# Scores' leaky relu into a PSUM bank, a new order of work by pairs of graphs, and a three-bank Strassen product in a four-layer graph attention kernel

## The chip, the cores and the metric

The kernel runs on one core of one Trainium2 chip. Its time is the device time of one launch in microseconds, the median of three runs. A profiled execution, taken by the hardware profiler, gives the views that are read below.

## The reference

128 independent graphs (`B = 128`) of 128 nodes each, with 512 features in float32, pass through four attention layers. Each layer adds its result to its input and normalises every row (`x = layernorm(x + layer(x))`). Layer 0 is plain attention on the features. Layer 1 has two parts: one with four heads over `x @ W1` (512 to 1024 columns) and an elu, and one with a single head over `h @ W2` (1024 to 512 columns). Layer 2 has eight heads over `x @ W` (512 columns). Layer 3 is attention on the features again. The scores of every attention have the same form:

```python
scores = leaky_relu(s_src[:, :, None] + s_dst[:, None, :], 0.2)
scores = where(adj == 0, -inf, scores)
attn   = softmax(scores)
out    = attn @ features
```

## The kernel before

**One graph fills the 128 partitions.** A graph is a tile of 128 x 512 floats. For each of them the kernel emits the same list of operations: `first` (layer 0), a projection by `W1`, `second` (the four heads), a share in the product by `W2` (`halves`), and `third` (the rest of layer 1, layer 2 and layer 3). All arithmetic is float32, and each float32 matmul appears in the trace as two records.

**An attention** is built of helpers. `spread` (L589 to L596) turns a column of scores into a row by way of DRAM and lays it out on all partitions: one write by SP, one read by SP. `attend` then runs, for each head, `prelu` on ScalarE (L646: leaky relu of row plus column, into the SBUF tile `z`), `masked` on VectorE (L654: the negated minimum of `z` plus a mask, with the row's minimum in `nm`), `exp` on ScalarE (L663, with the row's sum) and one reciprocal (L671). Some attentions are scaled on GpSimd (L673). `turned` (L607 to L622) transposes the result in blocks of 32 x 32 on VectorE and finishes the transposition by a write to DRAM and a read from it on SP's queue. Only then can TensorE use it: `mixed` (L725) for one head, L896 and L938 for several. Per graph there are six calls of `attend` with 1, 4, 1, 4, 4 and 1 heads, so 15 of each head's instruction. In the trace all SBUF tiles of 128, 512 or 1024 floats are named `w`, all PSUM banks `ps`.

**The product by W2** is done for two graphs at once by Strassen's scheme, with seven block products for eight. It uses four PSUM banks `pa` to `pd`, four evictions by ScalarE (L807) and four additions on VectorE (L812) for each pair; the sums of blocks are made on GpSimd (L780). Half of it is emitted with the odd graph of a pair and half with the even graph of the next pair.

**The order of the work** is set at build time. `plan` places one graph's operations in a cyclic timetable of `PERIOD = 28` us from rough costs (a DMA counts 7.06 us in it). `order` then runs a list scheduler over all graphs: on each engine it takes the operation that can start first, no further ahead than `AHEAD = 20` us of due time, and hands out PSUM banks (at most 8) and SBUF buffers by its own clock. Each engine, SP's DMA queue included, executes the resulting list strictly in order. The preparation of the weights (L295 to L560) is part of the same list, with due times up to 205 us.

Of the kernel before, what the change touches and what calls it, by code (L numbers as in the profile page):

```python
# [26 lines left out]

PERIOD = 28.0
LATENCY = {"PE": (0.0, 0.8), "DVE": (0.15, 1.44), "ACT": (0.1, 1.44), "POOL": (0.1, 1.44), "SP": (7.06, 7.06)}
FLOW = {"PE": (0.0, 0.6), "DVE": (0.15, 0.8), "ACT": (0.1, 0.8), "POOL": (0.1, 0.8), "SP": (4.5, 4.5)}
AHEAD = 20.0
URGENCY = 0.6
BANKS = 8

SEED, SPREAD = 989, 8.0


class Buf:


    def __init__(self, tag, shape, dtype=F32):
        self.tag, self.shape, self.dtype = tag, shape, dtype
        self.size = 1
        for d in shape[1:]:
            self.size *= d

        if dtype is F32 and shape[0] == P and self.size in (P, 4 * P, 8 * P) and not tag.startswith(("ps", "scr")):  # L50
            self.tag = f"w{self.size}"
        self.ap = self.slot = None

# [7 lines left out]
class Op:  # L61
    def __init__(self, engine, cost, emit, ins, outs, extra, uses=(), dma=0.0):
        self.dma = dma
        self.engine, self.cost, self.emit, self.extra = engine, cost, emit, extra
        self.wait = 0
        self.ins, self.outs = ins, outs
        self.uses = list(uses)
        self.bufs = list(dict.fromkeys([*ins, *outs, *uses]))

    def done(self, reader=None):  # L70
        own, other = LATENCY[self.engine]
        return self.cost + self.extra + (own if reader is self.engine else other)


class Pipeline:
    def __init__(self, make, n, place):
        self.make, self.n, self.place = make, n, place

    def plan(self, ops):


        before, after = [set() for _ in ops], [[] for _ in ops]
        last, readers = {}, {}
        for k, op in enumerate(ops):
            for b in op.ins:
                before[k].add(last[b])
            for b in op.outs:
                if b in last:
                    before[k].add(last[b])
                before[k].update(readers.get(b, ()))  # L90
            before[k].discard(k)
            for q in before[k]:
                after[q].append(k)
            for b in op.ins:
                readers.setdefault(b, set()).add(k)
            for b in op.outs:
                last[b], readers[b] = k, set()
        left = [0.0] * len(ops)
        for k in reversed(range(len(ops))):
            left[k] = ops[k].cost + max(  # L100
                (left[q] + ops[k].done(ops[q].engine) - ops[k].cost for q in after[k]), default=0.0
            )
        taken = {e: [] for e in LATENCY}
        times, ready, missing = [0.0] * len(ops), [0.0] * len(ops), [len(q) for q in before]
        waiting = [k for k in range(len(ops)) if not missing[k]]
        rng = random.Random(SEED)
        shift = [SPREAD * rng.random() for _ in ops]
        while waiting:
            k = min(waiting, key=lambda k: (ready[k] - URGENCY * left[k] + shift[k], k))
            waiting.remove(k)  # L110
            op, t = ops[k], ready[k]
            spans = taken[op.engine]
            while True:
                u = t % PERIOD
                clash = [
                    y + d - u for x, y in spans for d in (-PERIOD, 0.0, PERIOD)
                    if u < y + d - 1e-9 and x + d < u + op.cost - 1e-9
                ]
                if not clash:
                    break  # L120
                t += min(clash) + 1e-9
                assert t < ready[k] + 2 * PERIOD, "the period is too short"
            spans.append((t % PERIOD, t % PERIOD + op.cost))
            times[k] = t
            for q in after[k]:
                ready[q] = max(ready[q], t + op.done(ops[q].engine) + max(ops[q].wait, 0) * PERIOD)
                missing[q] -= 1
                if not missing[q]:
                    waiting.append(q)
        return times  # L130

    def run(self, setup):
        times, events = self.plan(self.make(None)), [(t, -1, k, op) for k, (t, op) in enumerate(setup)]
        for g in range(self.n):
            for k, op in enumerate(self.make(g)):
                if op is not None:
                    events.append((g * PERIOD + times[k], g, k, op))
        events.sort(key=lambda e: e[:3])
        for g, op in self.order(events):
            for b in op.outs:  # L140
                if b.ap is None and b.slot is not None:
                    b.ap = self.place(b, g)
            op.emit()

    def order(self, events):

        ops, n = [e[3] for e in events], len(events)
        ends, first, last, readers, open_uses = {}, {}, {}, {}, {}
        before, after = [0] * n, [[] for _ in ops]
        makes, coming = [[] for _ in ops], {}  # L150
        for i, op in enumerate(ops):
            need = {last[b] for b in op.ins + op.uses if b in last}
            for b in op.outs:
                need.update([last[b]] if b in last else [], readers.get(b, ()))
                if b not in first:
                    first[b] = events[i][0]
                    if b.tag != "const":
                        makes[i].append(b)
                        coming.setdefault(b.tag, []).append(i)
            need.discard(i)  # L160
            before[i] = len(need)
            for q in need:
                after[q].append(i)
            for b in op.ins + op.uses:
                readers.setdefault(b, []).append(i)
            for b in op.outs:
                last[b], readers[b] = i, []
            for b in op.bufs:
                open_uses[b] = open_uses.get(b, 0) + 1
                ends[b] = max(ends.get(b, 0.0), events[i][0] + op.done())  # L170

        free = {}
        for b, t in first.items():
            if b.tag != "const":
                places = free.setdefault(b.tag, [])
                s = next((s for s, e in enumerate(places) if e <= t), len(places))
                places[s : s + 1] = [ends[b]]
        assert len(free["ps"]) <= BANKS, "too few banks"
        free = {tag: [(0.0, s) for s in range(BANKS if tag == "ps" else len(p))] for tag, p in free.items()}
        ready, released, clock, lane = [0.0] * n, {}, {e: 0.0 for e in FLOW}, 0.0  # L180
        known = {e: [i for i in range(n) if not before[i] and ops[i].engine == e] for e in FLOW}
        issued, low, out = [False] * n, 0, []

        def start(i):
            t = max(clock[ops[i].engine], ready[i])
            for b in makes[i]:

                rank = 0
                for q in coming[b.tag]:
                    if q >= i or rank >= len(free[b.tag]):  # L190
                        break
                    rank += 1
                if rank >= len(free[b.tag]):
                    return None
                t = max(t, free[b.tag][rank][0])
            return t

        while len(out) < n:
            best = None
            for e, waiting in known.items():  # L200
                found = None
                for i in waiting:
                    if events[i][0] > events[low][0] + AHEAD and i != low:
                        break
                    t = start(i)
                    if t is not None and (found is None or t < found[0]):
                        found = (t, i)
                        if t <= clock[e]:
                            break
                if found and (best is None or found < best):  # L210
                    best = found
            t, i = best
            op = ops[i]
            known[op.engine].remove(i)
            issued[i] = True
# [6 lines left out]
            if op.engine == "POOL":  # L222
                other += op.extra
# [20 lines left out]
def tile_gat_stack(  # L244
# [86 lines left out]
    def spread_row(t, r, a):  # L331
# [5 lines left out]
        return b  # L337

# [700 lines left out]
```

## Time and profile before

| | before |
|---|---|
| median of 3 runs | 3231.36 us (3228.59 to 3233.77) |
| span of the profiled execution | 3258.4 us |
| instructions | 62058 |
| PE busy | 3066.8 us (94%) |
| DVE busy | 2779.0 us (85%) |
| ACT busy | 2451.2 us (75%) |
| POOL busy | 1895.1 us (58%) |
| DMA engines, mean | 186 GB/s |

The page gives no other time for the profiled execution than its span, which is 27 us (0.8%) above the median of the runs shown. PE is TensorE's matmuls, PEld its loads of weights, DVE is VectorE, ACT ScalarE, POOL GpSimd, SP the queue that issues nearly all transfers.

### The profile page before, as it was taken

The page shows a single profiled execution, that of the slowest core. Times are in us where ns is not written, and L with a number is a line of the kernel's source. Part 1 is how long each engine was busy: PE and PEld are TensorE (multiplying, and loading weights), DVE is VectorE, ACT ScalarE, POOL GpSimd, SP SyncE. Part 2 cuts the span into 40 slices and gives each one's busy share as a digit, 9 for nine tenths or more (in the row PEclk, how much of TensorE's full clock was granted, in tenths as well). Part 3 has the DMA queues.
Part 4 walks back from the last instruction along what each step waited for, and adds up shares of the span by engine and source line. Part 5 has one row for each costly group of instructions (what it writes and reads, how often), then busy time and mean ns, then how long its engine had stood idle before and what let it go on. Part 6 is the DMA issues. An engine that isn't in the chain of part 4 may idle for free. (4 is left out here: it accounts for less than half of the span.)

```text
span 3258.4 us, 62058 instructions
## 1 busy us (share of the span) xinstructions
PE 3066.8 (94%) x14822; PEld 2488.7 (76%) x14822; DVE 2779.0 (85%) x9833; ACT 2451.2 (75%) x8741; POOL 1895.1 (58%) x2347
## 2 busy tenths in 40 slices
PE   6899999999999999999999999999999999999984
PEld 4688887787777877877777778777787777878853
DVE  4779888888888988898888889889898898989875
ACT  2457787787777777787777877777877777778875
POOL 4655655665565655665555665565566556565533
PEclk7899999999999999999999999999999999999985
DMA  4358777877877877877778777877787787777875
GB/s 119 94 136 196 183 205 188 200 193 190 203 187 188 205 186 192 201 190 200 188 187 200 191 188 204 189 190 201 191 204 187 188 205 188 196 196 190 197 174 129
DMA packets 1657567, 606.08 MB, mean 186 GB/s; under 512 B 1311562, under 2 KB 1508170, under 8 KB 1657204
## 3 DMA queue, kind: packets, MB, share of 16 engines
q1 hardware_dynamic: 1655836, 598.97, 75.0%
q8 instruction: 120, 1.97, 0.2%
q14 instruction: 243, 1.99, 0.2%
q0 software_dynamic: 576, 2.10, 0.2%
q10 hardware_dynamic: 792, 1.06, 0.1%
HBM read 374.43 MB, written 227.48 MB: 185 GB/s over the span
## 5 line engine op out<-in xcount | busy, mean ns | idle before, releaser
L710 PE MATMUL ps<-w1s,w 128*128 128x258 f32 x4096 | 926.9, 384 | 48.5 <-DMA w<-scr 25.0
L710 PEld LDWEIGHTS ps<-w1s,w 128*128 128x128 f32 x4096 | 777.0, 191 | 186.3 <-DVE xl L812 39.5
L654 DVE CUSTOM_DVE_ANT_0 w<-w,w 128x128 f32<-128x128 f32 x1920 | 861.1, 544 | 65.6 <-ACT w L646 49.2
L794 PE MATMUL ps<-w2s,w 128*128 128x257 f32 x3584 | 849.0, 383 | 8.5 <-POOL w L780 8.4
L663 ACT ACTIVATE w<-w,nm 128x128 f32<-128x128 f32 x1920 | 748.0, 394 | 98.2 <-DVE nm L654 76.3
L794 PEld LDWEIGHTS ps<-w2s,w 128*128 128x128 f32 x3584 | 669.1, 191 | 188.8 <-issue 80.0
L646 ACT ACTIVATE w<-w,xl 128x128 f32<-128x128 f32 x1536 | 488.8, 389 | 279.9 <-DMA w<-row 259.1
L607 DVE STREAM_TRANSPOSE w<-w 128x512 f32<-128x512 f32 (+1 forms) x1024 | 551.5, 540 | 34.3 <-ACT w L663 13.3
L710 PE MATMUL ps<-wha,w 128*128 128x273 f32 x2048 | 502.3, 398 | 7.3 <-DMA w<-scr 6.9
L710 PEld LDWEIGHTS ps<-wha,w 128*128 128x128 f32 x2048 | 383.2, 192 | 87.4 <-DVE w L607 6.3
L699 ACT ACTIVATE w<-w,mr,rd 128x512 f32<-128x512 f32 x512 | 415.2, 811 | 33.9 <-POOL mr L692 33.0
L692 POOL TENSOR_SCALAR mr<-mv,rd 128x1 f32<-128x1 f32 x512 | 160.1, 313 | 409.4 <-ACT rd L686 201.8
L663 ACT ACTIVATION_READ_ACCUMULATOR w<-w,nm 128x1 f32 x1920 | 368.1, 192 | 0.0
L681 DVE BATCH_NORM_STATS2 st<-w 128x6 f32<-128x512 f32 x512 | 337.2, 668 | 5.4 <-POOL w L986 4.6
L881 POOL TENSOR_TENSOR xl<-xl,b1t 128x512 f32<-128x512 f32 x256 | 335.2, 1310 | 1.6
L938 PEld LDWEIGHTS ps<-xl,w 128*128 128x128 f32 x2048 | 274.3, 196 | 80.8 <-issue 24.4
L646 ACT ACTIVATE w<-w,sc 128x128 f32<-128x128 f32 x384 | 152.3, 397 | 227.6 <-DMA w<-row 226.6
L725 PE MATMUL ps<-w,w 128*128 128x512 f32 x512 | 277.4, 624 | 32.6 <-DMA w<-scr 31.6
L738 POOL TENSOR_SCALAR w<-adj 128x128 f32<-128x128 int32 x256 | 192.4, 752 | 188.2 <-DMA adj<-in_adj_dram 75.1
L717 ACT COPY xl<-ps 128x258 f32<-128x258 f32 (+1 forms) x768 | 273.2, 362 | 31.8 <-PE ps L710 31.3
L938 PE MATMUL ps<-xl,w 128*128 128x66 f32 x2048 | 265.2, 273 | 27.7 <-DMA w<-scr 14.4
L654 DVE DVE_READ_ACCUMULATOR2_ANT nm<- 128x1 f32 x1920 | 290.5, 151 | 0.0
(213 smaller groups left out, 4258.8 us busy)
## 6 DMA issues: line engine op xcount, KB each, us to landing
scr<-w SPq DMA_DIRECT2D x640, 256.0 KB
w<-scr SPq DMA_DIRECT2D x640, 256.0 KB
w<-row SPq DMA_DIRECT2D x128, 512.0 KB
w<-in_x_dram SPq DMA_DIRECT2D x128, 256.0 KB
w<-row SPq DMA_DIRECT2D x128, 256.0 KB
out_dram<-w SPq DMA_DIRECT2D x128, 256.0 KB
w<-row SPq DMA_DIRECT2D x384, 64.0 KB
scr<-w SPq DMA_DIRECT2D x384, 64.0 KB
```

Of the source, the lines that this page charges most:

```text
L607: op("DVE", 0.12 + 0.133 * n, lambda: nc.vector.transpose(zb.ap.rearrange("p b h c -> p h b c"), src.ap.rearrange("p (h b c) -> p h b c", ...
L646: nc.scalar.activation(z.ap[:, h, :], db.ap[:, h0 + h, :], AF.Prelu, bias=src(h0 + h), alpha=SLOPE)
L654: nc.vector.tensor_tensor_reduce(out=zz.ap[:, h, :].rearrange("p (b a) -> p a b", b=4), in0=z.ap[:, h, :].rearrange("p (a b) -> p a b", b= ...
L663: nc.scalar.activation(zz.ap[:, h, :], zz.ap[:, h, :], AF.Exp, bias=nm.ap[:, h : h + 1], scale=-1.0, accum_out=rs.ap[:, h : h + 1],)
L681: op("DVE", 0.6, lambda: nc.vector.bn_stats(st.ap, y.ap), [y], [st])
L699: op("ACT", 0.7, lambda: nc.scalar.activation(y.ap, y.ap, AF.Identity, bias=mr.ap, scale=rd.ap), [y, rd, mr], [y])
L710: op("PE", w * 4 / 2400 + 0.006, lambda k=k: nc.tensor.matmul(px.ap[:, :w], lhsT=lhs.ap[:, k, :], rhs=wa(k, c), start=(k == 0), stop=(k == ...
L717: op("ACT", 0.06 + w / 1200, lambda: nc.scalar.copy(dst(), px.ap[:, :w]), [px], [t])
L725: op("PE", width * 4 / 2400, lambda: nc.tensor.matmul(pa.ap[:, :width] if len(xv.shape) == 2 else pa.ap.rearrange("p (s c) -> p s c", s=2) ...
L794: return lambda: nc.tensor.matmul(q[b].ap[:, :C2], lhsT=x()[:, k, :], rhs=w2s[:, slot, k, :], start=(fresh and k == 0), stop=(k == 3), ski ...
L881: op("POOL", 1.3, lambda nh=nh: nc.gpsimd.tensor_add(xl.ap[:, nh, : 2 * FH], xl.ap[:, nh, : 2 * FH], b1t[:, nh * 2 * FH : (nh + 1) * 2 * F ...
L938: op("PE", 0.225, lambda u=u, h=h: nc.tensor.matmul(pa.ap[:, u * CH : (u + 1) * CH], lhsT=pt.ap[:, u, :], rhs=xl3.ap[:, h * CH : (h + 1) * ...
```

## The change

The change rewrites the scheduler and regroups the kernel by pairs of graphs. The arithmetic of the reference is the same. Its parts:

- `attend` writes the leaky relu to a PSUM bank (`z = bank()`), one bank for up to four heads, so that `masked` reads one operand from PSUM and the mask from SBUF.
- `strassen` takes the place of `halves`: the product by `W2` is emitted in one piece for a pair. `pa` accumulates on through four of the seven products, `pb` and `pc` take the rest. Three evictions and one final copy are on ScalarE, three additions on VectorE.
- `pair` emits two graphs together: both `first`, both projections, both `second`, one `strassen`, both `third`, both layer-2 projections, both `fourth`. The second graph of a pair is given a lag of half a period.
- `plan` and `lay_out` take the place of the class `Pipeline`. They have other costs: the four matmuls of one accumulation are one operation, a transfer lands 1.7 + 0.6 us plus its own transfer time after its issue, at most 8 transfers are in flight, and VectorE operations marked `port` and GpSimd operations exclude each other. Due times are 49 us apart for each pair, and the scheduler looks 60 us ahead.
- The preparation of the weights has due times up to 111 us instead of 205 us.
- Small ones: `exp(h - 1)` of the elu is written in place of a tile of its own, and the last attention reads its transposed weights by the other of the two layouts in `turned`.

```diff
-PERIOD = 28.0
-LATENCY = {"PE": (0.0, 0.8), "DVE": (0.15, 1.44), "ACT": (0.1, 1.44), "POOL": (0.1, 1.44), "SP": (7.06, 7.06)}
-FLOW = {"PE": (0.0, 0.6), "DVE": (0.15, 0.8), "ACT": (0.1, 0.8), "POOL": (0.1, 0.8), "SP": (4.5, 4.5)}
-AHEAD = 20.0
-SEED, SPREAD = 989, 8.0
+PERIOD, PACE, AHEAD = 51, 49, 60
+HOP = {'PE': 0.5, 'DVE': 0.5, 'ACT': 0.5, 'POOL': 0.5, 'SP': 1.0}
+URGENCY, SEED, SPREAD = 0.6, 56445, 16.0
+BANKS, PRODUCTS = 8, 2
+FLIGHT, LANDS = 1.7, 0.6
+LANES = 8
...
-            z, zz, nm, rs, ri = (Buf(f"{t}{nh}", s) for t, s in (
-                ("z", [P, nh, P]), ("zz", [P, nh, P]), ("nm", [P, nh]), ("rs", [P, nh]),
-                ("ri", [P, nh])))
-            def prelu():
-                for h in range(nh):
-                    nc.scalar.activation(
-                        z.ap[:, h, :], db.ap[:, h0 + h, :], AF.Prelu, bias=src(h0 + h), alpha=SLOPE
-                    )
+        zz, nm, rs, ri = (Buf(f"{t}{nh}", s) for t, s in (
+            ("zz", [P, nh, P]), ("nm", [P, nh]), ("rs", [P, nh]), ("ri", [P, nh])))
+        z = bank()
+        zh = lambda h: z.ap[:, h * P : (h + 1) * P]
+
+        def prelu():
+            for h in range(nh):
+                nc.scalar.activation(zh(h), db.ap[:, h0 + h, :], AF.Prelu, bias=src(h0 + h), alpha=SLOPE)
...
                     nc.vector.tensor_tensor_reduce(
                         out=zz.ap[:, h, :].rearrange("p (b a) -> p a b", b=4),
-                        in0=z.ap[:, h, :].rearrange("p (a b) -> p a b", b=4),
+                        in0=zh(h).rearrange("p (a b) -> p a b", b=4),
...
+        product(pa, left[0][0], 0, True)
+        taken(pa, t1)
+        product(pc, left[0][1], 1, True)
+        added(pc, t1, 0, 0)
+        product(pa, s[1], 4, False)
+        product(pb, s[0], 3, True)
+        taken(pa, u2)
+        taken(pb, v)
+        product(pa, s[2], 5, False)
+        product(pb, s[3], 2, False)
+        added(pa, v, 1, 1)
+        added(pb, u2, 0, 1)
+        product(pa, left[1][1], 6, False)
+        copied(pa, wide, lambda: to(1, 0), joins=[out[1]])
...
+    def pair(n):
+        a, b = 2 * n, 2 * n + 1
+        sts = [first(a)]
+        k = len(ops)
+        sts.append(first(b))
+        for o in ops[k:]:
+            o.lag = PERIOD / 2
+        xl = [Buf("xl1", [P, 2, N1]) for _ in range(2)]
...
+        hT = [second(st, t) for st, t in zip(sts, xl)]
+        xl2 = [Buf("xl2", [P, 2, C2]) for _ in range(2)]
+        left = [[(t, lambda t=t: t.ap) for t in both] for both in hT]
+        strassen(left, sums(left, [P, 4, P]), w2s, 4, C2, slice(0, C2), lambda g, h: xl2[g].ap[:, h, :], xl2, w2_ready)
+        for g, st, t in zip((a, b), sts, xl2):
+            third(g, st, t)
...
+        for g, st, t in zip((a, b), sts, xl3):
+            fourth(g, st, t)
+
+    pairs = B // 2
+    offsets = None
+    for n in range(pairs):
+        begin = len(ops)
+        pair(n)
+        if offsets is None:
+            own = ops[begin:]
+            offsets = plan(own)
+        for o, t in zip(ops[begin:], offsets):
+            o.due = n * PACE + t
```

## The prediction

> **What bounds the kernel now.** I read the table of stages first, for where TensorE stands still.
>
> ```profile
> core 0: us, PE busy (x) PEld busy (x) DVE busy (x) ACT busy (x) POOL busy (x), PEclk, DMA share, GB/s
> 0.00:163.00 163.00, 124.17 (x448) 87.71 (x449) 97.80 (x287) 58.26 (x178) 96.65 (x103) 0.83 0.40 106
> 163.00:326.00 163.00, 160.80 (x794) 134.71 (x793) 134.21 (x439) 111.63 (x393) 89.05 (x102) 1.00 0.68 166
> 326.00:3095.00 2769.00, 2677.55 (x13201) 2191.98 (x13200) 2435.47 (x8692) 2172.62 (x7797) 1655.09 (x2056) 1.00 0.79 194
> 3095.00:3258.00 163.00, 104.26 (x383) 74.28 (x381) 111.52 (x419) 108.67 (x377) 54.27 (x87) 0.71 0.63 152
> ```
>
> A graph needs 115 matmul records (32 for W1, 28 for W2, 16 for layer 2, 16 and 16 for the heads, 6 for the three single-head attentions, one transpose). So the long stage, with 13201 records, holds 114.8 graphs: **24.12 us a graph, of which PE is busy 23.32 and idle 0.80**. The other engines have more slack (DVE 21.2 us, ACT 18.9, POOL 14.4 a graph). The kernel is bound by TensorE, and what an order of work can win is the 91.5 us of PE idle in this stage and what stands at the ends: 38.8 us of idle in the first 163 us, 2.2 in the second and 58.7 in the last, where the granted clock is also low (0.83 and 0.71).
>
> Next, the waits of PE in the long stage (line, releaser: total, times, longest):
>
> ```profile
> PE ps L710 <- DMA w<-scr: 25.0, 24, 2.1
> PE ps L725 <- DMA w<-scr: 15.2, 27, 1.3
> PE ps L850 <- DVE w L903: 15.0, 15, 1.9
> PE ps L710 <- DVE ri L671: 10.1, 10, 2.1
> PE ps L710 <- DVE st L681: 8.4, 5, 2.0
> PE ps L725 <- ACT w L663: 4.5, 6, 1.0
> PE ps L725 <- ACT xl L717: 4.1, 10, 0.7
> ```
>
> With four smaller rows, transfers end 40.2 us of it, DVE 36.6, ACT 10.1, POOL 1.4: 0.35, 0.32, 0.09 and 0.01 us a graph.
>
> Last, whether DVE works at its own speed. The group of the masked minimum, then one burst of it on the timeline with the GpSimd operation beside it:
>
> ```profile
> L654 DVE CUSTOM_DVE_ANT_0 w<-w,w 128x128 f32<-128x128 f32 x1920 | 861.1, 544 | 65.6 <-ACT w L646 49.2 <-DMA row<-w 11.2 <-ACT w L663 3.8
> ```
> ```profile
> L654 DVE CUSTOM_DVE_ANT_0 w<-w,w x1722: 328/383/1522, 325.9 to 3095.0; 128x128 f32<-128x128 f32 x192
> ```
> ```profile
> 1502.43 1.04 POOL L673 TENSOR_TENSOR w<-w,ri 128x512 f32<-128x512 f32 x1
> 1502.56 1.16 DVE L654 CUSTOM_DVE_ANT_0 w<-w,w 128x128 f32<-128x128 f32 x1
> ...
> 1503.57 0.15 DVE L654 DVE_READ_ACCUMULATOR2_ANT nm<- 128x1 f32 x1
> 1503.57 0.39 DVE L654 CUSTOM_DVE_ANT_0 w<-w,w 128x128 f32<-128x128 f32 x1
> ```
>
> The mean is 544 ns, the median 383, the longest 1522. The first head here took 1.16 us; it was let go when the GpSimd multiplication that began just before it ended (1503.47). The next one took 0.39.
>
> [...] No ACT write to PSUM is in this trace.
>
> **The change part by part.** (1) *prelu to PSUM*: 1920 instructions that took 389 to 397 ns. [...] ACT is idle 22% of the long stage, and 306.6 us of its waits before L646 from 800 to 2600 us are for the row transfer, so nothing reaches the end from this alone.
>
> (2) *Masked minimum from PSUM*: 1920 instructions lose the blocking, 544 - 383 = 161 ns each: -309 us of DVE. [...] I take -250, DVE at some 2500 us with (3). GpSimd is no longer blocked by these either: the masks from `adj` have a mean of 752 ns against a least of 645 (256 of them, 27 us), `mr` 313 against 254 (512, 30 us): up to -57 us of POOL, some of it due to DVE operations that keep two SBUF inputs (L744, L959). Neither engine bounds. What is bought is latency: DVE's 36.6 us of PE idle shrinks, and exp, the transpose and the transfer behind each masked minimum start earlier.
>
> (3) *Three-bank Strassen*: seven products as before, so 3584 records and the same PE time. Four evictions by ACT stay four (three and the last copy); DVE's four additions become three: 64 x 404 ns = -26 us, hidden. `pa` is now read three times between products that add to it; each read (359 ns on ACT, 404 on DVE) has another bank's product beside it, 8 records in 1.9 us on the timeline. Taken at nothing; if the order put no product between, 3 x 64 x 0.4 = +77 us. One bank of four is returned. The score tile takes one: a four-head burst of prelu and minimum ran from 1501.55 to 1504.42, so 3 x 2.9 and about 3 x 1 us a graph, half a bank on average. These cancel.
>
> (4) *SP's queue and the transfers*: the same 30 issues a graph: 8 writes and 8 reads of `turned`, 5 of each of `spread`, x, adj twice, out. At the medians of the trace (432, 429 to 639, 538, 423 ns) that is about 15 us of 24. The bytes stay, so their share goes from 0.79 to about 0.81 when the same work takes 2% less. All issues are moved past each other, and one that waits for its source holds all behind it: that is the risk in rival B.
>
> (5) *The order*: this is where time is won or lost. Of the 0.80 us a graph I expect the DVE part to fall from 0.32 to 0.08 by (2) and a scheduler that knows which operations exclude each other; the transfers from 0.35 to 0.14, as it prices each by its size and looks 60 us ahead, not 20; ACT and POOL stay at 0.08. Idle 0.30, pace 23.62: 0.50 x 115 = -57 us. At the head PE stood 9.0 us before 40 us, waiting for a mask, and 5.7 and 5.0 us at about 120 to 130 for a transfer and a block sum; with more work within reach I take -20 us of the 99.7 at the ends. The tail hardly moves: after the last Strassen two layers hang on single transfers (5.77, 3.86, 2.57 us on the chain that ended last), whatever the order. Bounds for the ends: -50 to +40 (two graphs now reach the tail together, and the second of a pair starts half a period late).
>
> Sum: -57 - 20 = -77 us on the span of 3258.4, so 3181. The median is 27 us below the span; I carry that difference over: **3155 us**. That is -2.4%; about 0.2% is what a measurement of this kernel can tell from no change.
>
> **The rivals.** *A, forecast*: 3155, chance 0.64. Its own range is 3090 (all 91.5 us of the long stage and 50 of the ends gone) to 3224.
>
> *B, the order trusts transfers that land too early* (slower). A row for eight heads is priced at 1.7 + 0.6 + 1.52 = 3.8 us from its issue; the chain at the end shows 5.77 in a stage where the engines are less busy. The narrow ones are priced right (3.96 against 3.86, 2.7 against 2.57). All engines run in order, so a row 2 us late holds ACT, and what is queued behind it, then `turned` and PE's next heads or projection. If two of a graph's thirteen transfers to SBUF that gate an engine are late by 2 us with a third of it uncovered, it is 2 x 2 x 0.33 = 1.3 us of idle a graph where A has 0.14 for transfers: pace 24.12 + (1.3 - 0.35) - 0.26 (A's gain on the other waits) = 24.81, +79 us on 115 graphs, less 10 at the head: 3300. It decides once PE's idle exceeds 0.97 us a graph (0.80 plus the 20 us of the ends). For it: `ACT w L646 <- DMA w<-row` is already the longest wait. Against: PE still ran at 97% with it. Chance 0.30.
>
> *C, no change*: DVE's relief is real, but every wait of PE that it shortens is followed by one for a transfer that lands no sooner (L710 already waits 24 times for `scr`, 1 us each), so the idle 0.80 us stays and is only put down to other releasers: 3225 to 3238. Chance 0.06.
>
> **How the numbers follow.** Faster 0.64, same 0.06, slower 0.30. The range runs from A's low end to B's value: 3090 to 3300.
>
> **What would show it.** Right: in the long stage 0.2 to 0.4 us of PE idle a graph; the masked minimum (now with `ps` as input) with a mean near 400 and its longest under 700 ns; DVE busy near 2500 us; still 3584 records of W2. Wrong: PE waits for `scr` or `row` transfers above 60 us, or a pace above 24.1. [...] if it falls and the pace doesn't, C holds.

## The result and the profile after

The kernel after takes **3494.3 us** (median, 3492.5 to 3499.3) beside 3230.0 for the kernel before on the same chip: a ratio of **1.084 [1.081, 1.087]**, slower by 264 us where 77 us less was forecast. The profiled execution has a span of 3490.5 us, 4 below the median.

The table of stages, cut as it was for the kernel before (first and second 163 us, the long stage, the last 163 us; columns in the first line, "x" counts instructions):

```profile
core 0: us, PE busy (x) PEld busy (x) DVE busy (x) ACT busy (x) POOL busy (x), PEclk, DMA share, GB/s
0.00:163.00 163.00, 124.72 (x442) 89.94 (x443) 92.29 (x290) 58.04 (x177) 92.98 (x102) 0.87 0.39 107
163.00:326.00 163.00, 153.43 (x719) 122.37 (x718) 117.62 (x430) 111.04 (x380) 82.39 (x97) 0.98 0.67 165
326.00:3327.00 3001.00, 2780.30 (x13246) 2183.34 (x13245) 2404.96 (x8660) 2295.03 (x7818) 1629.85 (x2062) 1.00 0.73 179
3327.00:3490.00 163.00, 102.43 (x421) 73.22 (x419) 103.75 (x391) 110.87 (x367) 57.07 (x88) 0.77 0.57 144
```

PE is still busy for 93% of the long stage. At 115 matmul records a graph the stage holds 115.2 graphs: **26.05 us each, against 24.12 before**. That is 1.93 x 115.2 = 222 us, nearly all of the 232 us by which the span grew. Idle time of PE is 1.92 us a graph (0.80 before). Its busy time rose too, from 23.32 to 24.14. Between 1000 and 3000 us PE stands still before 297 matmuls (3.9 a graph) instead of 94 (1.1). By the records of this trace a matmul after such a break adds 0.46 us to the busy time, and any other, which overlaps with the one before it, 0.20; 2.7 breaks more a graph are then some 0.7 us (an estimate from these figures), most of the rise. The busy share of DVE, ACT and POOL fell, and transfers fell from 0.79 to 0.73 of the time. So no other engine and no transfer path became the bound; all of them stand still for a larger part of the time.

The waits of PE in the long stage (line, releaser: total us, times, longest):

```profile
PE ps L838 <- DVE xl L747: 29.3, 22, 1.5
PE ps L702 <- DVE nm L650: 24.4, 26, 2.4
PE ps L702 <- DVE w L846: 19.3, 39, 1.5
PE ps L838 <- DVE nm L650: 18.4, 23, 1.2
PE ps L771 <- ACT ps L645: 16.9, 22, 1.4
PE ps L771 <- DVE z L884: 12.4, 10, 1.9
...
PE ps L702 <- DMA w<-scr: 2.8, 4, 0.9
```

Over all rows of this view DVE ends 155.1 us, ACT 45.8, transfers 4.1. Before, transfers ended 40.2, DVE 38.2 (the 36.6 of the prediction leaves out three small rows), ACT 10.1. The waits are many, short and on many lines: additions of `strassen` (L747), masked minimum (L650), elu (L846), leaky relu (L645), the evictions that divide by the row sums (L884).

The two groups that the change rewrites (line, engine, operation, shapes, count | busy us, mean ns | idle before and what ended it):

```profile
L645 ACT ACTIVATE ps<-w,xl 128x128 f32<-128x128 f32 x1536 | 564.2, 370 | 113.1 <-DMA w<-row 53.3 <-DVE w L846 7.3 <-DVE nm L650 6.5
L650 DVE CUSTOM_DVE_ANT_0 w<-ps,w 128x128 f32<-128x128 f32 x1920 | 548.4, 376 | 275.4 <-ACT ps L645 260.9 <-issue 5.6 <-POOL ae L802 2.4
```

and the masked minimum by its line between 1000 and 3000 us (shortest/median/longest ns):

```profile
L650 DVE CUSTOM_DVE_ANT_0 w<-ps,w x1155: 333/379/403, 1005.9 to 2996.4; 128x128 f32<-128x128 f32 x193
```

The masked minimum is what was promised: mean 376 ns instead of 544, longest 403 instead of 1522. But DVE now stands 260.9 us before it, waiting for the leaky relu (49.2 before).

Where a late input goes shows in the chain that ended last, in order of time (start us, us, what), around one attention:

```profile
2018.06 2.11 PE ps L702 x8
2020.17 0.85 PE ps L878 x8
2021.02 0.02 issue
2021.04 0.45 DVE z L884
...
2021.70 0.19 SPq L622
...
2021.98 3.94 DMA w<-row
...
2026.01 0.38 ACT ps L645
...
2027.22 0.38 ACT ps L645
2027.60 0.02 issue
2027.62 0.38 DVE w L650
```

That each piece starts within some hundredths of a microsecond of the end of the one before says nothing by itself: a chain is made by going back from each instruction to what released it. What it does say is on what the end depends. Here, in the middle of the kernel, one row transfer and four leaky relus stand on it, and not PE's own instructions. For the kernel before the same view leads back no further than its last 70 us, so the two chains can't be compared; experiment 6 has one that can.

### The profile page after: what moved, and what is told of

Same layout as the page of the kernel before. It is cut to its first block, busy times and chain, and to the rows that moved or that the text cites. A ratio compares the mean times of both kernels' runs of the same rounds, so it can differ in the third digit from the quotient of the medians.

```text
span 3490.5 us, 62293 instructions
## 1 busy us (share of the span) xinstructions
PE 3160.9 (91%) x14822; PEld 2468.9 (71%) x14822; DVE 2718.6 (78%) x9769; ACT 2575.0 (74%) x8741; POOL 1862.3 (53%) x2347
## 4 chain that ended last, share of the span: by engine, by line
PE 28%; DVE 22%; ACT 20%; DMA 14%; issue 6%; SPq 2%; POOL 1%; DVEq 0%; ACTq 0%; POOLq 0%
PE ps L702 21%; ACT ps L645 9%; DMA w<-row 9%; DVE w L650 6%; ACT w L659 5%; DVE st L676 4%; PE ps L771 3%; PE ps L878 3%; ACT w L693 2%; DVE w L779 2%; DMA scr<-w 2%; DVE w L617 2%; DVE w L846 1%; DMA row<-sT 1%; ACT xl L710 1%
## 5 line engine op out<-in xcount | busy, mean ns | idle before, releaser
L702 PE MATMUL ps<-w1s,w 128*128 128x258 f32 x4096 | 950.3, 387 | 37.1 <-DMA w<-scr 15.7
L702 PEld LDWEIGHTS ps<-w2s,w 128*128 128x128 f32 x3584 | 667.4, 192 | 184.0 <-issue 38.2
L650 DVE CUSTOM_DVE_ANT_0 w<-ps,w 128x128 f32<-128x128 f32 x1920 | 548.4, 376 | 275.4 <-ACT ps L645 260.9
L645 ACT ACTIVATE ps<-w,xl 128x128 f32<-128x128 f32 x1536 | 564.2, 370 | 113.1 <-DMA w<-row 53.3
L702 PE MATMUL ps<-wha,w 128*128 128x273 f32 x2048 | 526.0, 404 | 65.3 <-DVE w L846 14.4
L710 ACT COPY xl<-ps 128x258 f32<-128x258 f32 (+2 forms) x832 | 303.4, 367 | 225.6 <-PE ps L702 223.9
L686 POOL TENSOR_SCALAR mr<-mv,rd 128x1 f32<-128x1 f32 x512 | 144.8, 284 | 592.4 <-ACT rd L681 471.5
L725 POOL TENSOR_TENSOR w<-w,w 128x512 f32<-128x512 f32 x256 | 337.3, 1325 | 69.1 <-DVE w L846 31.2
L669 POOL TENSOR_TENSOR w<-w,ri 128x512 f32<-128x512 f32 (+1 forms) x256 | 195.5, 764 | 264.5 <-DVE ri L667 201.8
L680 ACT ACTIVATE rd<-mv,eps 128x1 f32<-128x1 f32 x512 | 147.5, 288 | 242.5 <-DVE mv L677 241.4
L838 PE MATMUL ps<-w,xl 128*128 128x128 f32 x2048 | 268.5, 280 | 59.4 <-DVE xl L747 30.7
```

Source lines behind the costliest of these rows:

```text
L645: nc.scalar.activation(zh(h), db.ap[:, h0 + h, :], AF.Prelu, bias=src(h0 + h), alpha=SLOPE)
L650: nc.vector.tensor_tensor_reduce(out=zz.ap[:, h, :].rearrange("p (b a) -> p a b", b=4), in0=zh(h).rearrange("p (a b) -> p a b", b=4), in1= ...
L702: nc.tensor.matmul(px.ap[:, :w], lhsT=lhs(k), rhs=rhs(k), start=(fresh and k == 0), stop=(k == nk - 1), skip_group_check=True,)
L710: op("ACT", 0.04 + w / 1200, lambda: nc.scalar.copy(to(), px.ap[:, :w]), [px], outs, joins)
L725: op("POOL", cost, lambda: nc.gpsimd.tensor_tensor(out=own[o][1](), in0=a[1](), in1=b[1](), op=what), [a[0], b[0]], [s[o]])
```

## The experiments

**Theories.** After the profile I held that the order of work was built on margins that are too short, a margin being the time that a scheduler leaves between the end of one operation and the start of another that needs its result. Two lines of the kernel after set it between engines; the excerpt of the change above does not have them:

```python
SEES = {"PE": 0.06, "DVE": 0.06, "ACT": 0.06, "POOL": 0.06, "SP": 0.0}
TAIL = {"PE": 0.165, "DVE": 0.09, "ACT": 0.1, "POOL": 0.05, "SP": 0.0}
```

Together that is 0.11 to 0.225 us, where the kernel before adds 0.6 to 0.8 us (`FLOW`). Transfers are taken to land 2.3 us and their own time after the start of their issue (`FLIGHT` and `LANDS`), where the kernel before counts 4.5 us and their own time from the end of the issue. Rivals: the leaky relu in PSUM (it may cost more than it brings), the price of this one operation (0.295 us in the order), the reuse of PSUM banks, the three-bank product, the longer look-ahead, the grouping by pairs, and plain luck of one order. All ratios are to the kernel before, with 95% intervals; "pace" is 115 x 2000 / (matmul records between 1000 and 3000 us), 24.20 us for the kernel before and 25.96 for the kernel after. The runs stand here by question; they were made in four rounds, and an expectation can speak of runs of the rounds before it.

**1. The leaky relu in PSUM alone, on the order rules of before** (`b_psum`). In the kernel before (shortened):

```diff
-        assert len(free["ps"]) <= BANKS, "too few banks"
...
+            z = bank()
...
-                        z.ap[:, h, :], db.ap[:, h0 + h, :], AF.Prelu, bias=src(h0 + h), alpha=SLOPE
+                        z.ap[:, h * P : (h + 1) * P], db.ap[:, h0 + h, :], AF.Prelu, bias=src(h0 + h), alpha=SLOPE
...
-                        in0=z.ap[:, h, :].rearrange("p (a b) -> p a b", b=4),
+                        in0=z.ap[:, h * P : (h + 1) * P].rearrange("p (a b) -> p a b", b=4),
```

> The kernel before with one part of the change alone: the leaky relu goes to a PSUM bank and the masked minimum reads it there. Its scheduler is left as it was and fits the bank requests in by its own clock. Theory 1: the blocking by GpSimd goes (masked minimum at a mean near 380 ns, DVE busy down by 150 us or more) and PE gains a little or nothing: 3180 to 3240 us. Theory 2: PE waits for banks, 3330 us or more. Theory 3: the old order hands out the bank freed longest ago, so no loss, 3180 to 3240 us.

Measured: 3191.6 us, **0.987 [0.984, 0.990]**, pace 23.59. Its groups:

```profile
L646 ACT ACTIVATE ps<-w,xl 128x128 f32<-128x128 f32 x1536 | 569.7, 371 | 208.9 <-DMA w<-row 163.7 <-DVE sT L588 3.5 <-DVE st L681 3.3
L654 DVE CUSTOM_DVE_ANT_0 w<-ps,w 128x128 f32<-128x128 f32 x1920 | 539.0, 375 | 174.1 <-ACT ps L646 170.6 <-ACT rd L686 1.2 <-ACT w L663 0.5
```

With the part by itself the kernel gains 1.3% and is faster than both. As the leaky relu now asks for a bank, the list scheduler also makes another order, and experiment 3 shows that an order alone can be worth 1%; so the sign is supported by experiments 2 and 7 too, the size is not. DVE's wait for ACT grew here too (170.6 us), and did no harm: PE's idle fell to 0.39 us a graph. That it fell because the masked minimum no longer loses time to GpSimd fits, but was not shown apart from the order.

**2. The kernel after with the leaky relu back in SBUF** (`a_sbuf`).

```diff
-        z = bank()
-        zh = lambda h: z.ap[:, h * P : (h + 1) * P]
+        z = Buf(f"z{nh}", [P, nh, P])
+        zh = lambda h: z.ap[:, h, :]
```

> The changed kernel with the leaky relu written to an SBUF tile again, as before; the order of every engine's instructions stays that of the changed kernel, because its scheduler never ran out of banks. Theory 1 (the new order counts on hand-offs between engines and on landings of transfers that are too short, so each engine reaches an instruction before its input is there): PSUM is not the cause, so this stays as slow or gets slower by the GpSimd blocking that comes back, 3490 to 3650 us, masked minimum at a mean over 480 ns. Theory 2 (score tiles in PSUM hold banks that TensorE then waits for): at least 100 us are won, 3250 to 3390 us, and the waits of PE for the masked minimum (65 us) are gone. Theory 3 (a freed bank is handed out again at once, last freed first): as theory 2, but smaller, 3400 to 3450 us.

Measured: 3555.0 us, 1.099 [1.097, 1.102], pace 26.57. Slower than after by 61 us: the part gains 1.7% in the new order too. Every engine has the same instructions in the same order in both traces, so this difference is that of the part alone. The masked minimum is slow again:

```profile
L650 DVE CUSTOM_DVE_ANT_0 w<-w,w 128x128 f32<-128x128 f32 x1920 | 827.5, 524 | 123.6 <-ACT w L645 111.9 <-DMA w<-scr 4.8 <-DMA scr<-w 1.0
```

So what costs 264 us stands elsewhere, and is some 320 us without this part (3555.0 beside 3234.4 for the kernel before in the same round).

**3. Smaller parts of the new order**, one at a time, in the kernel after:

```diff
# a_fifo: banks are taken in the order in which they came free
-        b.slot = max(fit, key=...)
+        b.slot = (min if b.tag == "ps" else max)(fit, key=...)
# a_true: the leaky relu priced as measured, and the first minimum placed after all four
-        op("ACT", [0.295] * nh, prelu, ...)
+        op("ACT", 0.4 * nh, prelu, ...)
# a_four: a fourth bank in the Strassen product (shortened)
+        taken(pa, u3)
...
-        product(pa, left[1][1], 6, False)
-        copied(pa, wide, lambda: to(1, 0), joins=[out[1]])
+        product(pd, left[1][1], 6, True)
+        added(pd, u3, 1, 0)
# a_ahead20: the look-ahead of before
-PERIOD, PACE, AHEAD = 51, 49, 60
+PERIOD, PACE, AHEAD = 51, 49, 20
# a_seed: another random order among equals
-URGENCY, SEED, SPREAD = 0.6, 56445, 16.0
+URGENCY, SEED, SPREAD = 0.6, 1, 16.0
```

> The changed kernel with one word altered: of the banks that are free, the one freed longest ago is handed out instead of the one freed last. The order of instructions is the same. Theory 3: TensorE no longer waits for evictions and masked minima of a bank's last user; PE idle in the long stage falls from 1.85 us a graph to about 1.0, so 3380 to 3420 us. Theory 1: the waits for the bank are a symptom, and most waits are for data; 3450 to 3500 us. Theory 2: little, 3440 to 3500 us.

> The changed kernel with one cost of its scheduler set to what the traces show: four leaky relus into one PSUM bank take 0.40 us each, not 0.295, and the first masked minimum starts only after the last of them, not after the first. Only the order of instructions changes. Theory 1a (this one cost is most of what the order gets wrong): DVE waits for ACT's leaky relu fall from 261 us to under 120, and the time to 3340 to 3400 us. Theory 1b (all hand-offs and landings are too short alike, the leaky relu is one of many): 3440 to 3490 us.

> The changed kernel with the Strassen product over four banks as before: the last product goes to a bank of its own, one eviction and one addition more in place of the last copy. Theory 1: the three banks are not the cause, 3470 to 3510 us. Theory S (the products that add to one bank wait for its three readings): PE idle before the products by W2 goes, 3400 to 3460 us.

> The changed kernel with the lookahead of its scheduler at 20 us in place of 60, all else as in the change. Theory A (the long lookahead lets the scheduler fill each engine with far work, so that an order with no room arises): most of the loss goes, 3270 to 3360 us. Theory 1 (allowances for hand-offs and landings): 3430 to 3510 us.

> The changed kernel with another random seed for its timetable (1 for 56445). All theories: within 2% of the changed kernel, 3430 to 3560 us; what it differs by is the luck of one order, against which the other differences must be read.

| kernel | us | ratio | pace |
|---|---|---|---|
| after | 3494.3 | 1.084 [1.081, 1.087] | 25.96 |
| a_fifo | 3481.8 | 1.076 [1.073, 1.080] | 26.14 |
| a_true | 3495.6 | 1.081 [1.078, 1.084] | 26.07 |
| a_four | 3535.2 | 1.093 [1.090, 1.096] | 26.37 |
| a_ahead20 | 3487.2 | 1.076 [1.072, 1.080] | 26.11 |
| a_seed | 3526.9 | 1.090 [1.084, 1.095] | 26.40 |

None of them moves it by more than 41 us, and none explains 264. A new random number alone moves it by 33 us. That is one draw and no measured spread, but it warns that a difference of about 1% between two orders says little of the edit (`a_fifo` keeps the order and moves only banks). I call it the luck of one order below. The price of the leaky relu is the clearest miss: with it right, DVE waited longer for it over the whole kernel, 354.0 us instead of 260.9:

```profile
DVE w L650 <- ACT ps L645: 354.0, 235, 5.4
```

**4. The margins of the order**, again in the kernel after:

```diff
-SEES = {"PE": 0.06, "DVE": 0.06, "ACT": 0.06, "POOL": 0.06, "SP": 0.0}
-FLIGHT, LANDS = 1.7, 0.6
-LANES = 8
...
# a_hand:   SEES PE 0.435, DVE 0.71, ACT 0.70, POOL 0.75
# a_land:   LANDS 3.3, LANES 16
# a_both:   SEES PE 0.25, others 0.35;  LANDS 2.0, LANES 12
# a_strong: SEES PE 0.435, others 0.7;  LANDS 2.0, LANES 12
```

> The changed kernel with longer hand-offs between engines alone in its scheduler (0.6 us from PE, 0.8 us from the others all told, as the scheduler before has them), transfers as in the change. Theory 1a: part of the gain of the run with both numbers altered, since a longer hand-off from ACT also covers the leaky relu: 3360 to 3420 us. Theory 1c (the landings of transfers are what is too short): 3450 to 3500 us.

> The changed kernel with later landings alone in its scheduler (a transfer is there 2.7 us later, 16 in flight), hand-offs as in the change. Theory 1c: 3300 to 3370 us. Theory 1a: PE hardly waits for transfers in the changed kernel, so little is won, 3430 to 3490 us.

> The changed kernel with two numbers of its scheduler altered: a hand-off between engines costs some 0.3 us more (PE 0.25, the others 0.35 us in place of 0.06), and a transfer lands 1.4 us later (2.0 in place of 0.6 us after its own time), 12 in flight. No instruction is added or taken away, only the order changes. Theory 1: the engines find their inputs ready; PE idle falls from 1.85 us a graph to about 1.0 and the PE busy time from 24.1 to 23.6, pace 24.6 us, so 3300 to 3360 us. Theory 2 and theory 3: the banks are used as before, so 3450 to 3520 us.

> The changed kernel with both allowances of its scheduler raised further than in the run with both: hand-offs 0.6 us from PE and 0.8 us from the others all told, landings 1.4 us later, 12 in flight. Theory 1 (too little slack behind what each engine waits for): better than the run with both smaller ones (3347 us), 3250 to 3320 us. Theory P (what is left over is the grouping by pairs, which sends two graphs into the same stage at once): no better, 3330 to 3400 us.

| kernel | us | ratio | pace |
|---|---|---|---|
| a_hand | 3437.3 | 1.061 [1.060, 1.063] | 25.70 |
| a_land | 3407.5 | 1.052 [1.051, 1.054] | 25.26 |
| a_both | 3347.0 | 1.036 [1.033, 1.040] | 24.74 |
| a_strong | 3387.2 | 1.047 [1.045, 1.050] | 25.33 |

Margins for engines alone win 57 us, for landings alone 87, both in a middling size 147. The first is under twice the luck of one order, the last over four times. Wherever `LANDS` was raised, `LANES`, the number of transfers allowed in flight, was raised with it, so that the longer flights don't hold back issues; the two were not tried apart. That a_strong, with larger margins, is worse than a_both was not expected: more margin isn't simply better.

**5. The mirror: short margins in the kernel before** (`b_short`). In the kernel before, without the change: only the margins of its list scheduler are cut. The first number of each pair, between two instructions of one engine, goes to zero as well, since the new scheduler has none there.

```diff
-FLOW = {"PE": (0.0, 0.6), "DVE": (0.15, 0.8), "ACT": (0.1, 0.8), "POOL": (0.1, 0.8), "SP": (4.5, 4.5)}
+FLOW = {"PE": (0.0, 0.225), "DVE": (0.0, 0.15), "ACT": (0.0, 0.16), "POOL": (0.0, 0.11), "SP": (1.9, 1.9)}
```

> The kernel before, leaky relu in SBUF as it was, with the hand-offs and landings of the changed scheduler in its list scheduler (0.11 to 0.225 us from engine to engine in place of 0.6 to 0.8, 1.9 us for a landing in place of 4.5). Theory 1 (short hand-offs make a tight order that the chip can't keep): slower, 3330 us or more, with the waits spread over all engines. The rival, that it is the grouping by pairs which makes the new order slow: this stays within 1.5% of the kernel before, 3190 to 3280 us.

Measured: 3441.0 us, **1.063 [1.060, 1.065]**, pace 25.71. The old scheduler, with the old grouping and the old Strassen product, loses three quarters as much once its margins are cut. So neither the grouping by pairs nor the new product is needed for such a loss. The place is another one, though. The waits of PE between 1000 and 3000 us:

```profile
PE ps L794 <- ACT u L807: 120.6, 37, 4.7
```

Here few, long waits for the Strassen product's copies carry most of the loss, where the kernel after has many short ones; the expectation, waits on all engines, missed that. The matmuls of that line also take 412 ns on average instead of 382, and the granted clock between 1000 and 3000 us is 0.97 instead of 1.00. How much of the loss goes with the clock was not separated.

**6. Margins and look-ahead together.** Still open was why a_strong stopped at 3387. My reading was that where the scheduler may look 60 us ahead, an operation that now seems late lets others pass that are not due for long, so that margins are paid for in disorder. No view shows this directly. The runs are a_strong with `AHEAD` 20 (`a_strong12`), and the same with `LANDS` 3.3, `LANES` 16, the leaky relu at 0.4 and `PERIOD` 54 (`a_strong20`). The second was made first, and the expectation of the other knew its time:

> The changed kernel with a lookahead of 20 us, hand-offs of 0.6 and 0.8 us all told and landings 1.4 us later, the leaky relu and the period as in the change. Both theories together: 3240 to 3300 us. If the later landings of 2.7 us or the leaky relu's true cost made the run at 3259 us, this stays above 3320 us.

> The same with the landings 2.7 us later and 16 in flight, the leaky relu at its measured 0.40 us, a period of 54 us, and the scheduler looking 20 us ahead as the one before does. Theory 1: the slack is now what the scheduler before has, so near the kernel before with the leaky relu in PSUM (3192 us), 3190 to 3270 us. Theory P: 3320 us or more in spite of the slack.

Measured: 3298.9 us, 1.019 [1.015, 1.023], pace 24.23; and 3258.6 us, 1.007 [1.005, 1.009], pace **23.72**. With pairs, the three-bank product, the new scheduler and its other prices all in place, the steady pace is better than before's and close to the 23.62 forecast. The rows between 1000 and 3000 us (columns as in the table of stages), of before:

```profile
1000.00:3000.00 2000.00, 1931.48 (x9505) 1579.52 (x9506) 1760.95 (x6285) 1567.30 (x5627) 1195.95 (x1486) 1.00 0.79 194
```

of after:

```profile
1000.00:3000.00 2000.00, 1857.21 (x8861) 1458.59 (x8860) 1614.76 (x5818) 1538.79 (x5249) 1092.35 (x1384) 1.00 0.73 180
```

of `a_strong20`:

```profile
1000.00:3000.00 2000.00, 1961.94 (x9695) 1607.89 (x9693) 1654.47 (x6373) 1667.43 (x5737) 1191.59 (x1516) 1.00 0.81 198
```

of `b_psum`:

```profile
1000.00:3000.00 2000.00, 1967.30 (x9749) 1621.23 (x9748) 1642.74 (x6419) 1657.49 (x5762) 1200.82 (x1520) 1.00 0.80 199
```

9695 matmul records against 8861 in the same 2000 us, with PE busy 1962 against 1857. The look-ahead alone did nothing (`a_ahead20`, 7 us), margins of this size alone 107 us (`a_strong`), the two together 195 (`a_strong12`). The chain that ended last says it as well; shares of the span by engine, first of after, then of `a_strong20`:

```profile
PE 28%; DVE 22%; ACT 20%; DMA 14%; issue 6%; SPq 2%; POOL 1%; DVEq 0%; ACTq 0%; POOLq 0%
```
```profile
PE 54%; DVE 19%; DMA 9%; ACT 8%; issue 5%; POOL 2%; SPq 1%; DVEq 0%; POOLq 0%; ACTq 0%
```

What keeps `a_strong20` behind `b_psum` by 67 us is in part its ends: 384 matmul records in its first 163 us and 310 in its last, against 468 and 360, that is 134 records or some 28 us at its pace.

**7. Margins and look-ahead with the old scheduler and the leaky relu in PSUM.** `b_psum_slack` is `b_psum` with `FLOW` at 0.8 (PE), 1.1 and 5.0 (SP); `b_psum60` is `b_psum` with `AHEAD = 60.0`.

> The kernel before with the leaky relu in PSUM, and its list scheduler's allowances raised: hand-offs 0.8 and 1.1 us, landings 5.0 us. Theory 1: a little more robust still, 3150 to 3192 us, since PE idles under 0.4 us a graph already. Theory P says nothing on it. If more slack only delays work, 3195 to 3230 us.

> The kernel before with the leaky relu in PSUM and a lookahead of 60 us in place of 20, its own allowances kept. Theory A: slower by 3% or more, 3290 us or more. Theory 1: the allowances protect it, 3170 to 3230 us.

Measured: 3215.1 us, 0.994 [0.992, 0.995], and **3187.9 us, 0.984 [0.980, 0.989]**, the fastest median of this study (its interval overlaps that of `b_psum`). So more margin than the old one costs a little, 23 us, within the luck of one order; and a long look-ahead is harmless in the old scheduler with its margins. Why it costs 88 us in the new one with margins nearly as long (`a_strong` against `a_strong12`) was not found. All three orders of the old scheduler with the leaky relu in PSUM lie below the kernel before, at 0.984 to 0.994.

## Why the prediction was wrong, step by step

**(1) Leaky relu to PSUM: wrong in sign.** The forecast counted on an ACT as busy as before or less; that was the author's estimate, and no trace had shown it. ACT went from 2451 to 2575 us busy; +77 of the +124 come with this part alone (`b_psum`: 2528). One instruction is shorter by 18 ns, on average 371 ns in `b_psum` against 389 before. Four in a row are not quicker: the hardware section below has the numbers. It lies beside other work, as forecast, and was not the cause of the loss.

**(2) Masked minimum: right.** Forecast a mean near 400, the longest under 700 ns, -250 us of DVE. Measured 376 and 403. That the forecast stayed below the 309 us which the blocking cost was the author's estimate of what an input from PSUM adds; no such addition shows (median 378 ns beside 383). With the part alone DVE's busy time falls from 2779 to 2532 (-247), and from 2961 to 2719 (-242) in the new order. With one SBUF input no minimum of the 1920 took over 403 ns, and the 1138 of them beside which GpSimd worked took 377 ns on average, the others 374. Before, with two, it was 691 ns (1522 at most) for the 1023 beside which GpSimd worked and 376 (404 at most) for the others. In the kernel after DVE's sum is only 60 us below before's, because the rest of the change costs it 182: the kernel with the leaky relu back in SBUF has 2961. Part of that is other instructions with two SBUF inputs: the small addition that had 638 ns on average has 984 in `a_sbuf` and 988 in the kernel after. It does not overlap with GpSimd more often (127 of 128 times before and after), but with another operation, here in the kernel after (start us, duration), both ending at 2022.74 to 2022.75:

```profile
2021.56 1.18 POOL L889 TENSOR_TENSOR w<-z,w 128x512 f32<-128x512 f32 x1 [0.48 <-DVE z L884]
...
2021.73 1.02 DVE L898 TENSOR_TENSOR sc<-sc,xl 128x2 f32<-128x2 f32 x1
```

POOL's sum fell by 33 us (up to 57 forecast). The blocking shows on its side too: before, `mr` (L692) took 379 ns on average beside the masked minimum and 265 beside none of the three operations L654, L744 and L959; in the kernel after (L686) it takes 264 beside the masked minimum. The masks from `adj` (L738) took 801 ns beside L744 and 668 beside none of the three. L959 did not lengthen `mr` (265).

**(3) Three-bank Strassen at nothing: holds.** 3584 records as said, and a fourth bank makes it no faster (+41 us, about the luck of one order).

**(4) Queue and transfers: the count held, the consequence not.** The share fell to 0.73, since all went slower; with the good pace of `a_strong20` it is the 0.81 forecast.

**(5) The order: this step failed.** I took 57 us off the pace; it added 222. (The parts of the 0.50 us a graph make 0.47, a matter of 3 us.) I reasoned that a scheduler that knows more (sizes of transfers, which operations exclude each other) gives a better order, and put a new price list down as a better one. What I did not do was to compare, constant by constant, what the two allow between an operation's end and its use: 0.6 to 0.8 us before against about 0.11 to 0.22 after. Each engine executes its list in order (in the trace of the kernel after, DVE's 9769 instructions and ACT's 6804 activations and copies follow it throughout), so an instruction whose input is later than the plan assumed holds everything behind it, and each such hold can make the next input late. The runs show both ways that the short margins are the main cause: margins put back bring the pace from 25.96 to 24.74 (`a_both`) or, with a short look-ahead and the other edits of `a_strong20`, to 23.72; margins taken from the old scheduler cost 6.3%. The hand-over itself does not look dearer than priced: in the two between engines on the chain above, from PE to DVE and from ACT to DVE, the next starts 0.02 us after the one before ends. My reading is that the longer margins leave room for inputs that are late for other reasons, such as the rows below and the leaky relus; no run tried this apart.

**The ends: forecast -20, measured about nothing.** First 163 us 442 records (448 before), second 719 (794), last 421 (383): 43 records less, 9 us.

**The 27 us carried over: also off.** I subtracted the distance of before's span to its median; after's span is 4 below its median. The miss of 339 us is made up of pace 57 + 222, ends 20 + 9, and this, 27 + 4.

**Rival B had the direction, not the mechanism or the size.** Landings priced later win 87 of the 264 us (`a_land`). But I looked for it in PE waits for `scr` and `row` above 60 us, and they are 4.1 us. On the chain that ended last, between 300 and 3320 us, stand 73 loads of a row: with one, four and eight heads they take 3.42, 4.44 and 4.02 us from issue (medians of 29, 18 and 26), where the order allows 2.55, 3.09 and 3.82 for one with no transfer ahead of it. By the same count the scheduler before allows 5.1, 5.7 and 6.5. The prediction doubted the row for eight heads; those for one and four heads exceed their price by more. A late row holds ACT, then DVE, and reaches PE as a wait for DVE, as in the chain above. A long wait of ACT for a row does no harm by itself, though; in the long stage it was three times as long before (first line) as after:

```profile
ACT w L646 <- DMA w<-row: 451.5, 306, 3.9
```
```profile
ACT ps L645 <- DMA w<-row: 153.0, 121, 3.6
```

And I saw only transfers, where the margins between engines had been cut even further. The sign "a pace above 24.1" was the one that caught it.

**What stays open.** Which of the last four edits brings a_strong12's 3299 to 3259 was not separated, nor why a_strong, with more margin than a_both, is slower by 40 us; the luck of one order is nearly as large. The rows measured above are those on the chain, so the late ones; how late the other transfers land was not measured. Of the prices of single operations only the leaky relu's was varied: the addition on L898 takes 988 ns on average, where it and the reduction before it are priced at 0.25 us together.

## What to carry to other kernels

When engines execute fixed lists in order, the constants of the tool that wrote the lists belong to the kernel: compare them one by one, and treat a shortened margin as a cost until a run shows otherwise, even where it is all that a hand-over takes. A new order and a local improvement are to be measured apart, for the small edit that gained 1.3% was buried under a new order that, without it, lost 10% (`a_sbuf`). And a wait is named after the last link of its chain: loads of rows are 9% of the chain that ended last here, while PE's waits for transfers are 4.1 us of 3001.

## What the runs showed of the hardware

Leaky relus into one PSUM bank did not overlap (none of the 1152 pairs of neighbours in a row of four in the kernel after), those into SBUF did (all 1152 before). The first line is ACT's timeline before (SBUF, start us, duration of the four), the second fence after (PSUM), on ACT and then on DVE:

```profile
1501.55 1.28 ACT L646 ACTIVATE w<-w,xl 128x128 f32<-128x128 f32 x4 [0.44 <-DMA w<-row]
```
```profile
2026.01 1.58 ACT L645 ACTIVATE ps<-w,xl 128x128 f32<-128x128 f32 x4 [0.43 <-DVE st L676]
...
2027.62 0.38 DVE L650 CUSTOM_DVE_ANT_0 w<-ps,w 128x128 f32<-128x128 f32 x1 [0.65 <-ACT ps L645]
```

In SBUF the four begin 292 ns apart and take 1.28 us; in PSUM some 403 ns apart and 1.58 us, though each is shorter (medians over the 384 rows of each trace). So PSUM was quicker for one instruction and slower for a row of four, which counts here.

The second thing: before, the first minimum began (1502.56) 0.27 us ahead of the end of the fourth leaky relu (1502.83). After, it begins at 2027.62, when all four are over (2027.60). It is the rule: between 1000 and 3000 us, of the first minima of four heads that waited over 0.15 us for a leaky relu, all 109 in the kernel after were let go by the fourth of their row; with SBUF it was the first, in 20 of 20 cases in the kernel before and in 25 of 28 in `a_sbuf`. With PSUM the first minimum above comes 0.02 us after the last write to its bank, though what it reads was written first; what makes it wait for the other three was not shown. So four heads in one bank gave up their overlap head by head. It was still a gain: in the same order of instructions the bank is worth 61 us (`a_sbuf` against after). Why the writes to PSUM did not overlap was not tried, nor four heads in four banks.
